# Earlier row loads, scatters in groups of four and later second-half gathers in a convolution-attention kernel

## The chip, the cores and the metric

The kernel runs on one core of a Trainium2 chip. A core has engines that run their own instruction streams: TensorE (PE; its weight loads are shown apart as PEld), VectorE (DVE), ScalarE (ACT) and GpSimd (POOL). SyncE (SP) issues most of the DMA transfers; ACT and POOL issue some. All of them wait for each other through semaphores. The metric is the device time of one launch in microseconds (us), the median of several runs.

## What is computed

The input `x` has 4 images of 32 channels, 128 x 128. Layer 0 is attention over channels: a space-to-depth step makes 128 x 4096 matrices `xs`, and

```
xs = space_to_depth(x)                       # per image: 128 channels, 4096 points
energy = einsum('bci,bcj->bij', q, q) / (d_i * d_j)      # 4096 x 4096, d: norms of the columns
out = gamma * einsum('bcj,bij->bci', q, softmax(energy)) + xs
```

Layer 1 works, image by image, on 4096 tokens of 128 numbers:

```
t = t + attention(layernorm(t))              # linear: Q (K^T V), summed over 8 heads
z = layernorm(t)
p = softmax(z @ router_w + router_b)         # 8 experts
top2, weights = top_k(p, 2), renormalised
t = t + sum_k weights[k] * (z @ expert_w[top2[k]] + expert_b)
```

All of it is in float32.

## The kernel before

**Images and steps.** The four images (0 to 3) run one after the other. `attend` walks the 4096 x 4096 score matrix of an image in tiles of 128 x 512, and only one triangle of it: row `i` of eight, columns `jc <= i`, four tiles each. One such tile is a **step**; an image has 144, counted here from 0 to 143. In a step PE makes the scores (L557, tile `pe`), ACT takes their exponent (L560, `pr`), PE multiplies an earlier `pr` with the values (L439, `po`), and the transposed share of an earlier tile is added with one more product (L374 or, for diagonal tiles, L395; `pg`). For that share DVE transposes 32 x 32 blocks (L368, L514, tile `F`) and the blocks are swapped by a trip through DRAM: SP issues one store (L482, L503) and six loads (L494). DVE adds the share to `o` (L384, L404).

**What is worked in between the steps.** The main loop keeps `clock`, which counts the work of the steps (12 for a full step; 4 to 10 for those of diagonal tiles), and `t`, the percentage of an image's 1568. It steps generators. Their instructions are put into the engines' queues in just this order, which is fixed for PE, DVE, ACT and SP; POOL's gathers, scatters and powers keep their program order as well.

- `prep(b, kc, st)` prepares a quarter `kc` of the rows of image `b`: it loads `xx` (four DMAs on SP, L278), transposes on PE into `ptq` (L312), copies to `qT` (L301, DVE), squares and sums (L323, L324), takes the power on POOL (`rn`, L163), scales (`qs`, L337) and transposes to `qn` (`ptn`, L345). It is listed in `timed` with a begin, an end and a count: in a step with `t` in reach it gets its next count if `done * (end - begin) < (t - begin) * count`. Each count resumes it twice, once before and once after the step's products. `idle(n)` yields 2n times, so n counts pass.
- `layer1(b, st)` of an image runs in the image after, in `steady`: one turn (two resumptions) per step, if `clock` has moved by 10 since its last turn. Image 3's is different: it has no sorting and finishes after the steps.

**Layer 1 in order.** `close_rows(kc)` divides the sums of a quarter of `o` (`den` L696, L701, PE `pbd` L723, L710, L732), takes the statistics (L735 and L631 to L637), a power on POOL (`rsa`, L163, and `nba`, L639), normalises on ACT (`xn`, L645) and adds to the Gram matrix (`pgram`, L677). The first quarter waits until the image before has set `sorted`. Then come `matrix`, `attention_rows` and `route`, and `sorted_experts(h)` for two halves of the tokens, which works in this order:

1. Scatter: 32 indirect DMAs of POOL write the half's token rows to `xs`, sorted by expert (L996), two to a turn. In half 1 two turns are left free after the 8th and after the 16th. Half 1 scatters when half 0 has "moved".
2. Products: after three free turns, pairs of tiles are loaded (L1022, SP), transposed (L1065), multiplied with the expert's weights (L1058, `pys`) and stored to `ys` (L1044, SP), in 25 turns. At their end half 1 sets `sorted`.
3. Gather: after one free turn, 32 indirect DMAs of POOL fetch the rows of `ys` into `yb` (L1123), two to a turn. Half 0 waits until half 1 has "moved", half 1 until half 0 has "gathered". Every fourth pair starts with a load of `acc` from DRAM on ACT's queue (L1099). DVE adds each gathered row four turns later (the combine, L1092), and every finished group of four is stored with four DMAs on SP (L1105).

Each scatter and gather also waits for the exponent of the step before it in the code (`wait_for(..., exps, ...)`), so that POOL doesn't run ahead. Counted in steps, half 0 scatters at 52 to 70, half 1 at 71 to 93; the products of half 0 go from 75 to 102, those of half 1 from 98 to 124; half 0 gathers at 104 to 121 and half 1 at 127 to 142. The `prep` calls of the next image load at steps 96 (`kc` 0) and 127 (`kc` 1) and transpose first at 101 and 130; `kc` 2 and 3 load at steps 4 and 47 of their own image.

The loop that paces it, as it stands (from L1339 on):

```
if b + 1 < B:
    nxt = states[b + 1]
    timed.append((prep(b + 1, 0, nxt), 65, 82, 13))
    timed.append((prep(b + 1, 1, nxt), 87, 99, 13))
...
        t = 100 * (clock[0] - start) / UNITS
...
        for n, (steps, begin, end, count) in enumerate(timed):
            if t >= begin and done[n] * (end - begin) < (t - begin) * count:
                moved.append(steps)
                done[n] += 1
```

Of the kernel before, what the change touches and what calls it, by code (L numbers as in the profile page):

```python
# [22 lines left out]
def kernel(  # L23
# [45 lines left out]
    B, C, H, W = x.shape  # L69
# [92 lines left out]
    def pow_neg_half(dst, src):  # L162
        pinned(nc.gpsimd.tensor_tensor(dst, src, neg_half.to_broadcast(list(src.shape)), ALU.pow))  # L163
# [13 lines left out]
    def idle(n):  # L177
        for _ in range(2 * n):
            yield

    def keep_running(n, pool=None, tag=None):

        bank = psum_t("spare") if pool is None else pool.tile([P, CH], F32, tag=tag, name="spare")
        for _ in range(n):
            nc.tensor.transpose(bank[:, :P], ident, ident)
# [4 lines left out]
    def hold(name, evict, alloc=psum_t):  # L190


        while len(held) >= banks[0]:
            held[0]()
        bank = alloc(name)

        def done():
            if done in held:
                held.remove(done)
                evict(bank)  # L200

        held.append(done)
        return bank, done
# [69 lines left out]
    def load_tokens(dst, b, k0, nk, queues=(nc.sync, nc.sync)):  # L273
        src = tokens(x, b)
        for r1 in range(2):
            for s in range(2):
                p0 = s * 64 + r1 * 32
                queues[r1].dma_start(dst[p0 : p0 + 32], src[s, r1, :, k0 : k0 + nk, :])  # L278


    def prep(b, kc, st):

        if b == 0:
            if kc == 0:
                st["all"] = big1.tile([P, 4, 8, HW2, 2], F32, tag="T", name="xx_0")
            xx = st["all"][:, kc]
        else:
            xx = xin.tile([P, 8, HW2, 2], F32, tag="xx", name=f"xx_{b}_{kc}")
        first = b == 0 and kc == 0
        load_tokens(  # L290
            xx.rearrange("p k w r -> p k (w r)"), b, 8 * kc, 8, (nc.sync, nc.scalar if first else nc.sync)
        )
        qT = qpool.tile([P, 2, NJ, P], F32, tag="qT", name=f"qT_{b}_{kc}")
        st.setdefault("qT", {})[2 * kc] = qT[:, 0]
        st["qT"][2 * kc + 1] = qT[:, 1]
        yield
        yield
        yield from idle(2 if b else 1)

        def load_half(g, pt):  # L300
            nc.vector.tensor_copy(  # L301
                qT[:, :, 2 * g : 2 * g + 2, :].rearrange("p s j (r c) -> p (j r) s c", c=64),
                pt.rearrange("p (m s c) -> p m s c", s=2, c=64),
            )

        for g in range(2):
            yield
            pt, done = hold(f"ptq_{b}_{kc}_{g}", partial(load_half, g))
            for jj in range(2):
                for r2 in range(2):  # L310
                    k = 4 * g + 2 * jj
                    nc.tensor.transpose(  # L312
                        pt[:, ts(2 * jj + r2, P)], xx[:, k : k + 2, :, r2].rearrange("p k w -> p (k w)"), ident
                    )
            yield
            done()
        yield
        yield
        ss = stat.tile([P, 2 * NJ], F32, tag="ss", name=f"ss_{b}_{kc}")
        rn = stat.tile([P, 2 * NJ, 1], F32, tag="rn", name=f"rn_{b}_{kc}")  # L320
        for s in range(2):
            sq = work.tile([P, NJ, P], F32, tag="qs", name=f"sq_{b}_{kc}_{s}", bufs=2)
            nc.vector.tensor_tensor(sq, qT[:, s], qT[:, s], ALU.mult)  # L323
            nc.vector.tensor_reduce(ss[:, ts(s, NJ)], sq, AX.X, ALU.add)  # L324
            if first:
                pow_neg_half(rn[:, ts(s, NJ), 0], ss[:, ts(s, NJ)])
            elif s == 1:
                pow_neg_half(rn[:, :, 0], ss)
            yield
            yield  # L330
        yield from idle(1)
        if first:
            keep_running(22, ps_g, "pg")
        scaled = []
        for s in range(2):
            qs = work.tile([P, NJ, P], F32, tag="qs", name=f"qs_{b}_{kc}_{s}", bufs=2)
            nc.vector.tensor_tensor(qs, qT[:, s], rn[:, ts(s, NJ)].to_broadcast([P, NJ, P]), ALU.mult)  # L337
            scaled.append(qs)
        for s, qs in enumerate(scaled):
            yield  # L340
            qn = npool.tile([P, CH], F32, tag="qn", name=f"qn_{b}_{2 * kc + s}")
            st.setdefault("qn", {})[2 * kc + s] = qn
            pt, done = hold(f"ptn_{b}_{kc}_{s}", lambda p, qn=qn: nc.scalar.activation(qn, p, AF.Copy))  # L343
            for j in range(NJ):
                nc.tensor.transpose(pt[:, ts(j, P)], qs[:, j, :], ident)  # L345
            yield
            done()
        yield
        yield
# [253 lines left out]
    def layer1(b, st):  # L603
# [9 lines left out]
        place = stat.tile([P, 2, KT], U32, tag="place", name=f"place_{b}", bufs=1)  # L613
        begin = stat.tile([P, 2, NT + 1], U32, tag="begin", name=f"begin_{b}", bufs=1)
        turns = [[], []]
        gate = first
        t2 = dram.tile([P, KT, D], F32, tag="t2", name=f"t2_{b}")
        keep = {}
# [302 lines left out]
        def sorted_experts(h):  # L921
# [66 lines left out]
            def offset(ap):  # L988
                return bass.IndirectOffsetOnAxis(ap=ap, axis=0)
# [4 lines left out]
            for n in range(2 * HR):  # L994
                k, i = r0 + n // 2, n % 2
                inst = nc.gpsimd.indirect_dma_start(xs[h], offset(place[:, i, k : k + 1]), xn[:, k, :], None)  # L996
                if not scatters:
                    pinned(inst)
                else:
                    tc.declare_no_dep(inst.ins, group=f"scatter_{b}_{h}", reason="no two tokens have the same place")  # L1000
                tc.add_to_no_dep_group(f"scatter_{b}_{h}", inst.ins)
                wait_for(inst.ins, xs_made[h] + xs_read[h], "what is replaced was made and read before")
                wait_for(inst.ins, exps, "not more of these at a time than steps have")
                scatters.append(inst.ins)
                if n % 2:
                    yield
                    yield
                if h == 1 and n in (7, 15):
                    yield from idle(2)
            turns[h].append("moved")  # L1010
            xs_made[h][:], xs_read[h][:] = scatters, []
# [68 lines left out]
                done()  # L1080
            if h == 1:
                st["sorted"] = True
            yield from idle(1)
            while "gathered" not in turns[0] if h == 1 else "moved" not in turns[1]:
                yield from idle(1)

# [244 lines left out]
    timed = [(first, 0, 1, 4)]  # L1331
    for b in range(B):

        if b == 0:
            for kc, begin, end in ((1, 0, 5), (2, 6, 20), (3, 25, 45)):
                timed.append((prep(0, kc, states[0]), begin, end, 12))
            timed.append((setup_weights(), 46, 58, 9))
            timed.append((setup_sorting(), 58, 98, 17))
        if b + 1 < B:  # L1339
            nxt = states[b + 1]  # L1340
            timed.append((prep(b + 1, 0, nxt), 65, 82, 13))
            timed.append((prep(b + 1, 1, nxt), 87, 99, 13))
        begin, end, count = (52, 94, 17) if b == 0 else (36, 47, 9)
        timed.append((input_rows(b, states[b]), begin, end, count))
        done = [0] * len(timed)
        start = clock[0]
        closing = None
        for half, _ in enumerate(chain(attend(b, states[b]), finish() if b == B - 1 else ())):
            if half % 2 == 0:
                t = 100 * (clock[0] - start) / UNITS  # L1350
                moved = []
                if closing is None and t > 84:
                    closing = layer1(b, states[b])
                    steady.append([closing.first_parts() if b == B - 1 else closing.all_parts(), clock[0]])
# [4 lines that stand above are left out]
                for stream in steady:  # L1359
                    if clock[0] >= stream[1]:  # L1360
                        stream[1] = clock[0] + PACE
                        moved.append(stream[0])
            for steps in moved:
                next(steps, None)
        for steps, *_ in timed:
            for _ in steps:
                pass
        timed = []
        if b + 1 < B:
            timed.append((prep(b + 1, 2, nxt), 2, 20, 13))  # L1370
            timed.append((prep(b + 1, 3, nxt), 30, 50, 13))
# [43 lines left out]
```

## Time and profile before

| what | us |
|---|---|
| median of 6 runs (1695.23 to 1698.42) | 1696.48 |
| the profiled execution's own time | 1699.35 |
| its span, first to last instruction | 1697.6 |
| PE busy in it | 1648.8 |
| DVE busy | 935.1 |
| ACT busy | 928.3 |
| POOL busy | 512.1 |
| first products of images 0, 1, 2, 3 | 13.8, 362.4, 767.6, 1171.2 |
| waits of PE for `xx` from DRAM (L312): 3, the longest | 11.5, 5.8 |
| waits of PE for `qs` of DVE (L345): 3, the longest | 7.8, 3.1 |
| waits of POOL's gathers (L1123) for a store of `ys` | 96.9 and 15.6 |

The mean granted clock of PE is 0.992 of full speed. 16 DMA engines moved 323.94 MB, a mean of 191 GB/s.

How to read it: the page gives the busy time of each engine, the span in 40 slices, the chain of work that ended last (each piece followed back to what released it) and the costliest groups of instructions. The timeline lists instructions in order of time: start, duration, engine, line, operation, output and input, and in brackets how long the engine stood idle before it and what ended that. The table by windows gives, for each stretch, its length, the busy time of PE, PEld, DVE, ACT and POOL with the number of instructions, the granted clock of PE (PEclk), the DMA share and GB/s. Times are us from the span's start. A product in float32 shows as two instructions.

### The profile page before, as it was taken

The numbers are of one execution on the slowest core, as the hardware profiler recorded it, in microseconds if no ns is written. First come the engines' busy times: TensorE is split into PE (matmuls) and PEld (weight loads), VectorE is DVE, ScalarE is ACT, GpSimd is POOL, SyncE is SP. The second block draws the span as 40 slices with busy tenths as digits, with TensorE's granted clock in tenths as the row PEclk, the third lists the DMA queues.
The fourth block names the chain that finished last, engine by engine and source line by source line (L and its number), as shares of the span: only waits on it lengthen the run. The fifth ranks groups of instructions, "written<-read, shape, count | busy, mean of one in ns | idle before, by whom it ended". The sixth has DMA issues, their size and how long they took to land.

```text
span 1697.6 us, 21941 instructions
## 1 busy us (share of the span) xinstructions
PE 1648.8 (97%) x5458; PEld 876.2 (52%) x5458; DVE 935.1 (55%) x2443; ACT 928.3 (55%) x2893; POOL 512.1 (30%) x553
## 2 busy tenths in 40 slices
PE   7999999999999999989999999999999999999898
PEld 4444444455554555545564455544555455554543
DVE  4434334467485335477468334557748633455686
ACT  3555445566565555546565555545557555554376
POOL 1000000011027425461014641544102742445167
PEclk9999999999999999999999999999999999999999
DMA  4554756754459778875457777886435876885001
GB/s 129 175 172 163 203 173 213 245 198 161 140 169 280 225 234 248 243 219 174 147 176 226 242 229 240 249 263 196 164 132 174 283 225 218 254 248 146 7 10 41
DMA packets 227341, 323.94 MB, mean 191 GB/s; under 512 B 31760, under 2 KB 155792, under 8 KB 213136
## 3 DMA queue, kind: packets, MB, share of 16 engines
q1 hardware_dynamic: 206704, 283.57, 52.8%
q0 software_dynamic: 12288, 25.19, 5.2%
q10 hardware_dynamic: 8224, 13.77, 2.8%
q8 instruction: 46, 0.75, 0.2%
q14 instruction: 79, 0.65, 0.1%
HBM read 152.28 MB, written 173.15 MB: 192 GB/s over the span
## 4 chain that ended last, share of the span: by engine, by line
PE 82%; DVE 7%; DMA 3%; ACT 3%; SPq 2%; issue 1%; POOL 1%; ACTq 0%; DVEq 0%; POOLq 0%
PE po L439 23%; PE pe L557 23%; PE pg L374 19%; PE pys L1058 3%; PE py L1207 2%; PE pg L395 2%; PE pys L1065 2%; PE pat L803 1%; PE pgram L677 1%; DMA F<-blocks 1%; ACT xn L645 1%; SPq L475 1%; PE ptq L312 1%; DVE F L368 1%; DVE df L710 1%
## 5 line engine op out<-in xcount | busy, mean ns | idle before, releaser
L560 ACT ACTIVATE pr<-pe 128x512 f32<-128x512 f32 (+1 forms) x576 | 322.6, 560 | 542.3 <-PE pe L557 501.3
L439 PE MATMUL po<-pr,qT 128*128 128x512 f32 (+3 forms) x1152 | 551.8, 561 | 3.9 <-ACT o L444 3.4
L557 PE MATMUL pe<-qn,qn 128*128 128x512 f32 x896 | 461.2, 596 | 2.0 <-ACT pr L560 1.7
L374 PE MATMUL pg<-F,qT 128*128 128x512 f32 x864 | 442.5, 594 | 1.9 <-DMA F<-blocks 1.2
L368 DVE STREAM_TRANSPOSE F<-pr 128x512 f32<-128x512 f32 x440 | 306.1, 702 | 150.4 <-ACT pr L560 137.3
L439 PEld LDWEIGHTS po<-pr,qT 128*128 128x128 f32 x1152 | 216.3, 191 | 250.9 <-issue 221.0
L379 ACT ACTIVATE junk<-F 128x512 bf16<-128x512 f32 x432 | 267.8, 620 | 2.1 <-DMA F<-blocks 1.3
L374 PEld LDWEIGHTS pg<-F,qT 128*128 128x128 f32 x864 | 164.4, 191 | 195.4 <-issue 178.5
L1123 POOL DMA_INDIRECT yb<-ys,place x192 | 186.0, 969 | 242.3 <-DMA ys<-xn 96.9
L996 POOL DMA_INDIRECT xs<-xn,place x192 | 186.1, 969 | 157.0 <-ACT pr L560 93.4
L557 PEld LDWEIGHTS pe<-qn,qn 128*128 128x128 f32 x896 | 154.3, 191 | 109.4 <-issue 101.6
L384 DVE TENSOR_TENSOR o<-o,pg 128x512 f32<-128x512 f32 x110 | 75.5, 686 | 205.7 <-PE pg L374 205.5
L163 POOL TENSOR_TENSOR rn<-ss,neg_half 128x8 f32<-128x8 f32 (+1 forms) x17 | 26.9, 1585 | 332.7 <-DVE ss L324 332.6
L560 ACT ACTIVATION_READ_ACCUMULATOR pr<-pe 128x1 f32 x576 | 111.9, 194 | 0.0
L1032 ACT ACTIVATE xn<-pys 128x256 f32<-128x256 f32 x120 | 45.3, 378 | 107.8 <-PE pys L1065 107.6
L163 POOL TENSOR_TENSOR rsf<-dm_f,neg_half 128x8 f32<-128x8 f32 (+1 forms) x15 | 26.2, 1748 | 233.7 <-DVE sv_f L637 233.7
L1058 PEld LDWEIGHTS pys<-ew_sb,xn 128*128 128x128 f32 x468 | 69.6, 191 | 46.5 <-issue 43.5
L557 PE MATMUL pe<-qn 128*128 128x512 f32 (+3 forms) x256 | 90.9, 438 | 0.7 <-ACT qn L343 0.7
L163 POOL TENSOR_TENSOR rsa<-dm_a,neg_half 128x8 f32<-128x8 f32 x16 | 26.4, 1649 | 192.0 <-DVE sv_a L637 191.6
L379 ACT ACTIVATION_READ_ACCUMULATOR junk<-F 128x1 f32 x432 | 82.6, 191 | 0.0
L1041 DVE COPY xn<-pys 128x256 f32<-128x256 f32 x60 | 25.4, 424 | 87.9 <-ACT xn L1032 86.4
L1041 DVE COPY result<-pys 128x256 f32<-128x256 f32 (+1 forms) x60 | 24.6, 410 | 88.2 <-ACT xn L1032 82.9
(216 smaller groups left out, 1670.8 us busy)
## 6 DMA issues: line engine op xcount, KB each, us to landing
blocks<-F SPq DMA_DIRECT2D x108, 1024.0 KB
F<-blocks SPq DMA_DIRECT2D x216, 192.0 KB
F<-blocks SPq DMA_DIRECT2D x216, 128.0 KB
xn<-xs SPq DMA_DIRECT2D x114, 128.0 KB
F<-blocks SPq DMA_DIRECT2D x216, 64.0 KB
below<-F SPq DMA_DIRECT2D x31, 384.0 KB
out_dram<-acc SPq DMA_DIRECT2D x128, 64.0 KB
xx<-in_x_dram SPq DMA_DIRECT2D x62, 128.0 KB
```

The lines of the kernel that those rows point to most:

```text
L163: pinned(nc.gpsimd.tensor_tensor(dst, src, neg_half.to_broadcast(list(src.shape)), ALU.pow))
L368: f()
L374: nc.tensor.matmul(pg.rearrange("p (a f) -> p a f", a=4), st["qT"][i][:, ib, :], G[:, :, ib], start=(ib == 0), stop=(ib == NJ - 1),)
L379: nc.scalar.activation(junk, G[:, :, ib], AF.Copy, accum_out=st["sums"][:, NJ * i + ib, jc : jc + 1])
L384: nc.vector.tensor_tensor(o, o, pg.rearrange("p (a j c) -> p a j c", a=4, c=S), ALU.add)
L439: nc.tensor.matmul(row["po"][:, lo:hi], qT[blk // NJ][:, blk % NJ, :], w, start=start, stop=(row["left"] == 0))
L557: nc.tensor.matmul(pe[:, c0:], qn[jc][:, ts(j, P)], qn[i][:, c0:], start=True, stop=True)
L560: nc.scalar.activation(pr[:, c0:], pe[:, c0:], AF.Exp, accum_out=sums[:, t, i : i + 1]).ins
L996: inst = nc.gpsimd.indirect_dma_start(xs[h], offset(place[:, i, k : k + 1]), xn[:, k, :], None)
L1041: nc.vector.tensor_copy(result[:, :n], p[:, 2 * P : 2 * P + n * D].rearrange("p (j c) -> p j c", c=D))
L1058: nc.tensor.matmul(p[:, 2 * P + j * D : 2 * P + j * D + D], bufs[4 + g % 2][:, j, :], weights[:, bass.ds(begins[2 * (g % 2) + j], D)], sta ...
L1123: inst = nc.gpsimd.indirect_dma_start(yb[k // 4][:, i, k % 4, :], None, ys, offset(place[:, i, k : k + 1]))
```

## The change

The whole diff:

```diff
@@ prep
         yield
         yield
-        yield from idle(2 if b else 1)
+        yield from idle((6 if kc < 2 else 2) if b else 1)
@@ layer1
         turns = [[], []]
+        paced = b < B - 2
         gate = first
@@ sorted_experts, scatter
                 if n % 2:
                     yield
                     yield
-                if h == 1 and n in (7, 15):
+                if paced and n % 4 == 3:
+                    yield from idle(1)
+                elif h == 1 and n in (7, 15):
                     yield from idle(2)
@@ sorted_experts, before the gather
             if h == 1:
                 st["sorted"] = True
-            yield from idle(1)
+            yield from idle(4 if paced and h == 1 else 1)
             while "gathered" not in turns[0] if h == 1 else "moved" not in turns[1]:
                 yield from idle(1)
@@ main loop
-            timed.append((prep(b + 1, 0, nxt), 65, 82, 13))
-            timed.append((prep(b + 1, 1, nxt), 87, 99, 13))
+            timed.append((prep(b + 1, 0, nxt), 60, 82, 17))
+            timed.append((prep(b + 1, 1, nxt), 83, 99, 17))
```

It does three things. The first two quarters of the next image's rows begin four counts earlier and have four more counts between their load and their first transposes. In layer 1 of images 0 and 1 (which run in images 1 and 2) the scatters of both halves go in fours, with one free turn after each four; this replaces half 1's two pauses of two turns. And in the same two images the second half's gathers have four free turns ahead of them instead of one. No instruction is added or removed on any engine; layer 1 of images 2 and 3 keeps its own pacing.

## Prediction

> **What bounds the kernel now.** I read the page first: PE is busy for 1648.8 of 1697.6 us, and 82% of the chain that ended last is PE. So a transfer or a DVE operation counts only where PE stands still for it, and I listed the gaps between PE's instructions. After the start and before the last image's tail only four exceed 1.2 us: 3.49 and 3.07 us in image 1, 2.19 and 3.07 us in image 2, each time at the same two steps. The chain of waits through image 1's two (start, us, what):
>
> ```profile
> 710.53 0.87 PE pe L557 x2
> 711.43 4.46 DMA acc<-t
> 716.34 0.43 SPq L278
> ...
> 719.11 5.08 DMA xx<-in_x_dram
> 724.32 0.72 PE ptq L312 x4
> ...
> 748.08 0.61 DVE qs L337
> 748.74 0.66 PE ptn L345 x4
> ```
>
> Steps are score tiles, 0 to 143 in each image; a step begins with its product L557, and what stands in which step is counted from the code's order and matched with the trace, instruction by instruction. The load of the next image's rows (L278) is issued in the code at step 127 (PE at 710.4), but SP issues it at 716.34, after a wait that the chain puts down to the landing of a gather's `acc<-t`; it lands at 724.2, and the transposes of step 130 wait. Later the transposes of step 137 wait for `qs`, because DVE is full: in 742 to 749 it is busy 6.86 of 7 us. PE's timeline shows what one gap costs:
>
> ```profile
> 719.80 1.02 PE L374 MATMUL pg<-F,qT 128*128 128x512 f32 x2
> 724.32 0.72 PE L312 MATMUL ptq<-ident,xx 128*128 128x128 f32 x4 [3.49 <-DMA xx<-in_x_dram]
> 724.87 1.15 PE L557 MATMUL pe<-qn,qn 128*128 128x512 f32 x2
> 725.81 1.91 PE L439 MATMUL po<-pr,qT 128*128 128x512 f32 x2
> 730.47 1.02 PE L439 MATMUL po<-pr,qT 128*128 128x512 f32 x2
> ```
>
> The pair at 725.81 takes 1.91 us against 1.02: the granted clock (PEclk, the third figure from the end) is 0.61 there.
>
> ```profile
> 718.00:725.00 7.00, 3.51 (x12) 1.66 (x11) 0.01 (x1) 1.30 (x4) 4.46 (x5) 1.00 1.05 294
> 725.00:729.40 4.40, 4.40 (x10) 1.75 (x9) 3.20 (x7) 1.30 (x4) 1.92 (x2) 0.61 0.99 268
> ```
>
> So a stall is priced by step lengths, from one L557 start to the next. A full step takes 2.58 us (729.61 to 732.19), four transposes 0.47 or 0.44 more. Steps 130 and 131 of image 1 take 11.52 (718.09 to 729.61) and should take 6.10: **5.42** lost. Steps 137 and 138 take 10.57 (742.93 to 753.50) and should take 5.60: **4.97**. Image 2's same steps lose 4.09 and 4.83. Image 0, with no gather, loses nothing there. Together **19.3 us** of 1697.6.
>
> **Part 1: the loads.** `prep` gets two turns per count. The transposes come at turn 8 now and at turn 16 after, that is at count 4 (t > 87 + 3x12/13 = 89.77) and at count 8 (t > 83 + 7x16/17 = 89.59): both are step 130 (t = 90.05). The load goes from the first step with t >= 87 (127) to the first with t >= 83 (121; t = 83.42): six steps ahead of where it was, PE at 694.7 instead of 710.4. Its four issues (0.43 to 1.19 us) pass SP's F<-blocks, ys and out_dram issues of those steps. SP's issues lag their step's start in PE by 5 to 12.7 us there, and issue to landing was 7.9 us (716.3 to 724.2), so the rows are there by 715.3 at the latest, and the transposes wanted them at 720.8. The load of the first quarter moves from step 96 to 89 and is not waited for now. Value: -5.42 and -4.09, nothing in images 0 and 3. What passed SP before it now comes up to 3.3 us later; the tightest swapped tile behind it (F_1_7_1) is issued 5.4 us before its product, and steps 125 to 129 get longer by 0.66 us each because the products move there (below): nothing.
>
> **Part 2: the scatters.** Layer 1 of the image before has one turn per step; steps of diagonal tiles, which move the clock by less than 10, give none. 32 scatters take 24 turns instead of 16 (half 0) and 20 (half 1). Half 0's products and gathers come 8 turns later, half 1's products 12. The instructions are the same; the POOL issues (0.96 us + 0.30) were not waited for. In place of gathers and products of steps 104 to 127 I get the same mix at 113 to 137; its precedent in the trace, beside the first quarter's transposes at 101 to 115, left no PE gap over 0.2 us. Value: 0.
>
> **Part 3: the second half's gathers** start 8 + 4 + 3 = 15 turns later: not at step 127 but at 142, and run to step 20 of the next image; combines run from step 5 to 26 instead of 131 to 5 of the next image. Also `close_rows(0)` of the next layer waits for `sorted`, 12 turns later: its first row (L696) goes from step 133 to 138. From steps 133 to 137 this takes six combines (0.34 each), the four L710 (2.78), L732 (1.22), eight L735 (1.6) and more: at least 7 us of a DVE that was 3.07 us late. Value: -4.97 and -4.83.
>
> **What they meet.** This cover is given back at the head of the next image, where `prep(.,2)` and `close_rows(2)` and `(3)` run. POOL keeps program order, and this order at step 19 is `rn`, a pair of gathers, `rsa`. Now, without gathers:
>
> ```profile
> 813.27 1.64 POOL L163 TENSOR_TENSOR rn<-ss,neg_half 128x8 f32<-128x8 f32 x1 [15.69 <-DVE ss L324]
> 815.02 1.64 POOL L163 TENSOR_TENSOR rsa<-dm_a,neg_half 128x8 f32<-128x8 f32 x1
> 816.97 1.65 ACT L645 ACTIVATE xn<-T,nba,rsa 128x128 f32<-128x128 f32 x4 [0.69 <-POOL nba L639]
> 818.86 1.05 PE L677 MATMUL pgram<-xn 128*128 128x128 f32 x8
> ```
>
> The four `xn` end at 817.46 to 818.62, and the four products that read one each start from 818.86 to 819.53: the last has 0.91 us of slack. The pair costs POOL 2 x (0.96 + 0.30) = 2.52, from these rows:
>
> ```profile
> 716.42 0.95 POOL L1123 DMA_INDIRECT yb<-ys,place  x1 [0.30 <-issue]
> 717.68 0.96 POOL L1123 DMA_INDIRECT yb<-ys,place  x1 [0.30 <-issue]
> ```
>
> It waits behind `rn`, and `rn` waits for DVE, which is nearly full there (the third busy figure):
>
> ```profile
> 795.00:805.00 10.00, 10.00 (x48) 6.72 (x47) 7.77 (x21) 7.99 (x27) 1.93 (x3) 1.00 0.49 147
> 805.00:815.00 10.00, 10.00 (x28) 4.71 (x27) 9.63 (x27) 3.99 (x13) 1.64 (x1) 1.00 0.52 180
> 815.00:825.00 10.00, 10.00 (x43) 6.26 (x42) 4.19 (x13) 7.58 (x26) 1.84 (x2) 1.00 0.64 219
> ```
>
> Six pairs of combines (0.70 each, 4.2) come between 789 and 811; idle time of DVE that takes them up is 2.06 before L404 at 801.6, little else: DVE is about 2.2 us late at `ss`. Stall at that `pgram` (step 21): 2.52 + 2.2 - 0.91 = **3.8**. Bounds: 1.6 if DVE isn't late, 0 if the pair is not in that place, 6.0 if the combines ahead of `rsa` and slower gathers (1.50 at 745.2) add 2.2. I take 3.8, since the order and the full DVE are both in the rows. The restart at the lower clock cost 1.93, 1.90, 1.90 and 1.76 in the four stalls (loss less gap): **1.9**. And `close_rows(0)` now reaches its `pgram` at step 1 of the next image, which lasts only 0.87 us; its DVE rows added up from step 140 on bring the last `xn` about 0.6 us too late: **0.6** (0 to 2). New cost at one boundary 6.3, at two 12.6.
>
> A rule that speaks against the restart term is in the Trainium skill, "TensorE: Matmul & The Clock Gate", Part 1: the clock is halved after an idle window of some 3.4 us. The trace differs: a gap of 2.19 us in image 2 was followed by a granted clock of 0.66 (1128 to 1133). By the page none of these gaps below 3.4 us would be followed by a restart; with my 3.8 us the sum is the same by both, and at the bound of 1.6 us it would be 3.8 us better.
>
> **Sum** for the profiled execution: 1699.35 us (span 1697.6) - 19.3 + 12.6 = 1692.7. It is 2.9 above the median of the runs, 1696.48, so the median goes to 1689.8, or **1690**.
>
> **Rivals.** (a) The two stalls go and nothing takes their place: POOL has issued the pair before `rn`, or DVE has room. For it: image 0 to 1 shows the same close_rows without any stall. Against: the pair's order and 0.91 us of slack. -19.3: 1677, up to 1683 with small stalls. (b) **Slower**: at the head of the next image the collision that is seen now at step 127 comes back. The third quarter's load (issued at 780.1, transposes at 793.6) gets no longer lead, and `acc<-t` of the moved gathers now stands before it in SP's waits. At 7.9 us to landing it may be 5.6 us later than now; SP is 4.9 us behind PE there, so it decides from 10.5 us behind, and 12.7 was reached at step 128. Price 5.42 per boundary on top of my forecast: -19.3 + 12.6 + 10.8 = +4.1, 1701. (c) The load is issued earlier in the code but not in time, because SP is behind: it would need over 18 us of lateness (694.7 to 712.9), and 12.7 is the most seen; the 9.5 stay, and the sum is +2.8: 1699.
>
> **Chances.** Forecast 0.50 (1683 to 1697; above 1693.1 it is within 0.2%, about what a measurement of this kernel can tell from no change), (a) 0.26, (b) 0.20, (c) 0.04. Faster by over 0.2%: 0.36 of the forecast's 0.50 + 0.26 = 0.62. Within: 0.13 + 0.04 = 0.17. Slower: 0.01 + 0.20 = 0.21. The range takes in (a) and most of (b): 1676 to 1702.
>
> **What would show it.** Right: no gap before L312 at step 130 nor before L345 at step 137 of images 1 and 2; L278 issued some 15 us earlier; gathers of half 1 until 50 us into the next image; a PE gap before `pgram` L677 near step 21 there, its `xn` waiting for `nba`, with a pair L1123 between the two L163. Wrong: that gap is missing (then 1677), or there is one before L312 near step 10 (then 1701).

## The result, and the profile after

| | median, us | runs |
|---|---|---|
| before | 1698.40 (1692.88 to 1703.31) | 71 |
| after | 1698.78 (1694.45 to 1703.83) | 31 |

The ratio is 1.0002, with a 95% interval of 0.9996 to 1.0009: no change that can be measured. The profiled executions stand the same way: 1699.12 us after (span 1697.3) and 1699.35 before (span 1697.6). Part of the miss is the base: the 1690 was reckoned from the median of six runs, 1696.48; over 71 runs it is 1698.40. The rest is the forecast gain of 6.7 us, which did not come.

In the changed kernel the line numbers of `layer1` behind the scatter's new branch are three higher (gather L1126, combine L1095, row load L1025, `acc` load L1102), those ahead of it one higher (scatter L997, `xn` L646, `pgram` L678).

**The four old gaps are gone.** PE's timeline of the changed kernel at steps 129 to 131 of image 1 (start, us, what; in brackets the idle time before it and what ended it):

```profile
717.64 0.61 PE L1061 MATMUL pys<-ew_sb,xn 128*128 x4
719.65 0.44 PE L1068 MATMUL pys<-ident,xn 128*128 128x128 f32 x2 [1.40 <-DMA xn<-xs]
...
722.50 0.63 PE L312 MATMUL ptq<-ident,xx 128*128 128x128 f32 x4
```

The transposes of `xx` (L312) start without a wait; before, there were 3.49 us ahead of them. But one step earlier stands a wait that was not there: 1.40 us for `xn<-xs`, a row load of the second half's products, which now run in these steps. The load of 128 KB took 6.79 us (the chain of waits has it from 712.82), in a window (714 to 721) with a DMA share of 1.02 and 348 GB/s; the clock stays at 1.00 behind this gap (721 to 725.4), where it was 0.61 behind the old one. At step 137 the transposes L345 follow the product before them without a gap, and in image 2 it is the same:

```profile
744.71 1.02 PE L374 MATMUL pg<-F,qT 128*128 128x512 f32 x2
745.57 0.60 PE L345 MATMUL ptn<-ident,qs 128*128 128x128 f32 x4
```

**The head of image 2 pays, as predicted.** POOL's timeline after, at steps 19 to 21:

```profile
810.84 1.71 POOL L163 TENSOR_TENSOR rn<-ss,neg_half 128x8 f32<-128x8 f32 x1 [5.30 <-DVE ss L324]
812.73 1.01 POOL L1126 DMA_INDIRECT yb<-ys,place  x1 [0.19 <-issue]
814.05 0.95 POOL L1126 DMA_INDIRECT yb<-ys,place  x1 [0.30 <-DVE F L368]
815.02 1.82 POOL L163 TENSOR_TENSOR rsa<-dm_a,neg_half 128x8 f32<-128x8 f32 x1
```

The pair of gathers stands between the two powers. PE then waits 2.75 us for the last `xn`, and the L439 pair behind it takes 1.32 us instead of 1.02:

```profile
817.78 2.08 PE L678 MATMUL pgram<-xn 128*128 128x128 f32 x8 [2.75 <-ACT xn L646]
...
820.50 1.32 PE L439 MATMUL po<-pr,qT 128*128 128x512 f32 x2
```

By the table of windows DVE is full from 795 to 815 (9.82 and 9.60 of 10 us, where it had been 7.77 and 9.63). In the window after that PE, the first busy figure, has 7.25 us, and its clock is 0.83:

```profile
815.00:825.00 10.00, 7.25 (x32) 5.75 (x32) 3.54 (x14) 6.29 (x22) 4.08 (x4) 0.83 0.89 271
```

**Image 0 pays too, which was not predicted.** SP's timeline, first before, then after:

```profile
232.76 0.42 SPq L482 DMA_DIRECT2D blocks<-F  x1
233.23 8.66 SPq L278 DMA_DIRECT2D T<-in_x_dram  x4
242.05 3.76 SPq L494 DMA_DIRECT2D F<-blocks  x6
```

```profile
232.92 8.19 SPq L278 DMA_DIRECT2D xx<-in_x_dram  x4
241.21 0.40 SPq L482 DMA_DIRECT2D blocks<-F  x1
...
247.29 3.23 SPq L494 DMA_DIRECT2D F<-blocks  x6
```

The four `xx` issues of the load for image 1 take 8.19 us of SP, because they wait there for a transfer `xs<-in_x_dram` of ACT's queue (the chain of waits has 3.02 us of it from 237.76). The kernel before has the same stop, but in the load of `T`, which stands behind the store `blocks<-F`. The store `blocks<-F` of step 101's tile is issued 8.5 us later than before, its loads 5.2 us later, and PE stands still:

```profile
253.74 1.31 PE L374 MATMUL pg<-F,qT 128*128 128x512 f32 x2 [1.89 <-DMA F<-blocks]
254.84 1.92 PE L557 MATMUL pe<-qn,qn 128*128 128x512 f32 x2
```

**The balance.** The same products in both profiled executions, after less before, give by stretch:

| stretch | predicted, us | measured, us |
|---|---|---|
| image 0 | 0 | +3.3 |
| image 1, steps 125 to 143 among them | -10.4 | -9.0 |
| head of image 2 | +6.3 | +6.9 |
| rest of image 2 | -8.9 | -8.1 |
| head of image 3 | +6.3 | +7.1 |
| rest of image 3 and the end | 0 | -0.4 |
| sum | -6.7 | -0.2 |

### The profile page after: what moved, and what is told of

Its sections match the earlier page's. It is cut to its first block, busy times and chain, and to the rows that moved or that the text cites. A ratio compares the mean times of both kernels' runs of the same rounds, so it can differ in the third digit from the quotient of the medians.

```text
span 1697.3 us, 21930 instructions
## 1 busy us (share of the span) xinstructions
PE 1648.3 (97%) x5458; PEld 876.2 (52%) x5458; DVE 934.3 (55%) x2443; ACT 927.9 (55%) x2893; POOL 511.9 (30%) x553
## 4 chain that ended last, share of the span: by engine, by line
PE 77%; DVE 7%; DMA 7%; ACT 3%; SPq 3%; issue 2%; POOL 1%; ACTq 0%; DVEq 0%; POOLq 0%
PE po L439 22%; PE pe L557 21%; PE pg L374 18%; PE pys L1061 3%; PE py L1210 2%; DMA blocks<-F 2%; PE pg L395 2%; DMA F<-blocks 2%; SPq L494 2%; PE pys L1068 1%; PE pgram L678 1%; DMA xn<-xs 1%; PE pat L804 1%; DVE F L368 1%; SPq L475 1%
## 5 line engine op out<-in xcount | busy, mean ns | idle before, releaser
L439 PE MATMUL po<-pr,qT 128*128 128x512 f32 (+3 forms) x1152 | 550.6, 560 | 3.3 <-ACT o L444 2.9
L557 PE MATMUL pe<-qn,qn 128*128 128x512 f32 x896 | 459.6, 595 | 1.9 <-ACT pr L560 1.6
L439 PEld LDWEIGHTS po<-pr,qT 128*128 128x128 f32 x1152 | 215.8, 191 | 249.8 <-issue 219.8
L997 POOL DMA_INDIRECT xs<-xn,place x192 | 185.0, 964 | 222.3 <-ACT pr L560 164.6
L1126 POOL DMA_INDIRECT yb<-ys,place x192 | 186.5, 971 | 202.0 <-ACT pr L560 62.9
L557 PEld LDWEIGHTS pe<-qn,qn 128*128 128x128 f32 x896 | 153.0, 191 | 103.6 <-issue 96.7
L1061 PEld LDWEIGHTS pys<-ew_sb,xn 128*128 128x128 f32 x468 | 69.9, 191 | 48.5 <-issue 46.4
L557 PE MATMUL pe<-qn 128*128 128x512 f32 (+3 forms) x256 | 91.1, 439 | 0.7 <-ACT qn L343 0.7
L1061 PE MATMUL pys<-ew_sb,xn 128*128 x468 | 71.6, 274 | 0.0
```

Of the source, the lines that this page charges most:

```text
L439: nc.tensor.matmul(row["po"][:, lo:hi], qT[blk // NJ][:, blk % NJ, :], w, start=start, stop=(row["left"] == 0))
L557: nc.tensor.matmul(pe[:, c0:], qn[jc][:, ts(j, P)], qn[i][:, c0:], start=True, stop=True)
L1061: nc.tensor.matmul(p[:, 2 * P + j * D : 2 * P + j * D + D], bufs[4 + g % 2][:, j, :], weights[:, bass.ds(begins[2 * (g % 2) + j], D)], sta ...
L1126: inst = nc.gpsimd.indirect_dma_start(yb[k // 4][:, i, k % 4, :], None, ys, offset(place[:, i, k : k + 1]))
```

## The experiments

**The theory** at the start: each part has its own effect, as the prediction priced it, plus the two costs just seen. **The rival**: the parts stand in for each other; a gap goes when the gathers move, whatever is done to the load. In an expectation, A and B are that run's own. The runs came in three groups of four, each with runs of the kernel before beside it (medians 1707.73, 1708.23 and 1697.73 us); the first two groups ran on one chip, the third on another, and a kernel is compared with others of its chip alone. The kernel before has a trace from the recorded runs only, so its gaps and times below are from there. In the table the microseconds are differences of medians; the ratio, with its interval, need not be the quotient of the medians (0.9929 stands for 12.1 us where the medians differ by 13.8).

| kernel | scatters | gathers | loads | against before, us | ratio (95%) |
|---|---|---|---|---|---|
| the changed kernel | new | new | new | +0.4 | 1.0002 (0.9996 to 1.0009) |
| the same, again | new | new | new | +0.4 | 1.0009 (0.9997 to 1.0020) |
| loads only | old | old | new | +2.7 | 1.0013 (0.9998 to 1.0027) |
| scatters only | new | old | old | -8.0 | 0.9957 (0.9941 to 0.9974) |
| gathers only | old | new | old | -9.5 | 0.9945 (0.9933 to 0.9958) |
| loads and scatters | new | old | new | -7.3 | 0.9962 (0.9948 to 0.9975) |
| scatters and gathers | new | new | old | -1.8 | 0.9991 (0.9978 to 1.0004) |
| loads of image 1 as before | new | new | new from image 2 | -1.2 | 0.9992 (0.9976 to 1.0008) |
| one free turn at step 19 | new | new | new | -7.0 | 0.9959 (0.9945 to 0.9973) |
| pause of 9 turns | new | new | new | -8.2 | 0.9950 (0.9932 to 0.9968) |
| the same, old loads | new | new | old | -13.8 | 0.9929 (0.9907 to 0.9951) |
| pause of 12, scatters alone | new | old | old | -11.1 | 0.9936 (0.9924 to 0.9948) |
| pause of 16, scatters alone | new | old | old | -10.9 | 0.9942 (0.9928 to 0.9956) |

"New" is as in the change, "old" as in the kernel before; a pause is in the second half's gathers.

**The loads alone.**

```diff
-        paced = b < B - 2
+        paced = False
```

> Only part 1 of the change (the two loads); scatters and gathers keep their old turns. Theory A (the stalls are additive and each belongs to its own part): the gaps at steps 130/131 of images 1 and 2 go (-5.4 and -4.1), those at steps 137/138 stay (4.97 and 4.83), the heads of images 2 and 3 have no new gap, and image 0 shows the gap for the block tile at step 101 (+3.8): in all -5.7 us against the kernel before, about 1692.7. Theory B (the earlier load helps only because the paced scatters also took the acc<-t transfers out of its way): a gap before L312 at step 130 stays, and the time is -1 to +4 us against before.

Measured: +2.7 us, 1.0013 (0.9998 to 1.0027). Each is right in one half: the gap before L312 goes, as A has it, but its time doesn't come back, and the result lies in B's range. SP's timeline around the load, first in the kernel before, then with the loads alone:

```profile
709.45 2.75 SPq L494 DMA_DIRECT2D F<-blocks  x6
715.96 0.34 SPq L482 DMA_DIRECT2D blocks<-F  x1
716.34 3.25 SPq L278 DMA_DIRECT2D xx<-in_x_dram  x4
```

```profile
703.52 2.40 SPq L278 DMA_DIRECT2D xx<-in_x_dram  x4
...
716.13 2.66 SPq L494 DMA_DIRECT2D F<-blocks  x6
```

The load is issued at 703.5 and is in good time. But SP's stop before 716 us stays: the chain puts it down to the landing of `acc<-t`, now ahead of F<-blocks instead of ahead of the load. So PE waits for the block tile, at almost the same place:

```profile
721.78 1.10 PE L374 MATMUL pg<-F,qT 128*128 128x512 f32 x2 [2.58 <-DMA F<-blocks]
```

In image 2 that gap is 3.31 us; step 137 of image 1 now waits 4.78 us for `qs` (3.07 before), that of image 2 2.33. The wait belonged to the queue and not to the load.

The instruction records of the trace also show why SP waits for a transfer that ACT issued. The 1577 transfers that SP and ACT issue signal their landing on eight semaphores, 100 to 107, which this program gives out in turn; an issue first waits (1443 of them do so in the trace of the kernel before) until the transfer that had its semaphore before it has landed. In the kernel before, `acc<-t` (issued at 711.43) has 107. The eighth transfer after it in the program, the store `blocks<-F` just ahead of the load, has 107 again: it goes out at 715.96, 0.07 us after `acc<-t` has landed, and the load behind it. With the loads alone the first of the F<-blocks transfers has the semaphore of `acc<-t`. The stop in image 0 is of the same kind: the fourth `xx` issue has the semaphore of `xs<-in_x_dram`. So which instruction is stopped depends on the order of all these transfers, and a change that moves some of them moves the stop.

**The scatters and the later gathers, loads as before.**

```diff
-        yield from idle((6 if kc < 2 else 2) if b else 1)
+        yield from idle(2 if b else 1)
...
-            timed.append((prep(b + 1, 0, nxt), 60, 82, 17))
-            timed.append((prep(b + 1, 1, nxt), 83, 99, 17))
+            timed.append((prep(b + 1, 0, nxt), 65, 82, 13))
+            timed.append((prep(b + 1, 1, nxt), 87, 99, 13))
```

> Only parts 2 and 3 (free turns of scatters and second-half gathers); the loads stay where they were. Theory A: the gaps at steps 137/138 go (-9.8), steps 130/131 still wait for xx (about 9.5 stay), image 0 loses nothing, the heads of images 2 and 3 pay 7.0 each as in the changed kernel: +4 us against before, up to +7 if the wait for the products' own loads at step 129 is also there. Theory B (the late load was an effect of the second half's gathers alone): no gap at step 130 either, and the time is about -5 us against before.

Measured: -1.8 us, 0.9991 (0.9978 to 1.0004). B is right about the gap: at step 130 only 0.48 us in image 1 is left, none in image 2, with the load at its old place. Why it goes is seen with the scatters alone, below: SP still stops for an `acc<-t` in the middle of the load. The time is above B's -5, because the heads cost more on this chip than B had counted with: 3.83 and 3.90 us of gap at step 21, and 0.95 and 0.92 before `pgram` at step 14 (the expectations below call it step 12), where the recorded trace of the changed kernel had none.

**The changed kernel again**, as the base on that chip:

> The changed kernel once more, as the base for the others on this chip. Both theories: within 2 us of the kernel before, with a gap at step 101 of image 0 (1.5 to 2 us), gaps for the products' loads at step 129 (0.8 to 1.9) and before pgram at step 21 of images 2 and 3 (2.75 to 3.9).

Measured: +0.4 us, 1.0009 (0.9997 to 1.0020), with gaps of 1.80 us at step 101 of image 0, 1.25 and 0.31 at step 129, 3.92 and 3.90 at step 21, as expected. The earlier loads make it 2.8 us slower than the kernel just above (1708.67 against 1705.90).

**The scatters alone.** Beside the loads of before:

```diff
-            yield from idle(4 if paced and h == 1 else 1)
+            yield from idle(1)
```

> Only part 2, the free turns of the scatters; the loads and the free turn ahead of the second half's gathers are as before. Everything of layer 1 behind the scatters comes 8 to 12 turns later all the same, sorted too. Theory A (this shift alone takes the gathers' acc<-t out of the way of the load at step 127 and the combines out of the way of close_rows): gap at step 130 at most 0.5 us, none at step 137, no pair between rn and rsa at step 19, a gap of 1.5 to 2.5 us before pgram at step 21: -4 to -8 us against before. Theory B (the parts do what the prediction put down to each: scatters nothing, loads steps 130/131, later gathers steps 137/138): gaps of over 2 us at 130 and 137 stay, and the time is that of before within 2 us or more.

Measured: -8.0 us, 0.9957 (0.9941 to 0.9974): this run's A in the time, and with it the rival. Gaps at step 130 are 0.72 and 0.35 us, none is at step 137. That part had been put at zero. But A's reason for step 130 is not what the trace shows: `acc<-t` is not out of the load's way. The four issues of the load, which take 3.25 us in the kernel before, take 6.70, because the second one waits for an `acc<-t` of the first half's gathers, which have moved there:

```profile
707.89 6.70 SPq L278 DMA_DIRECT2D xx<-in_x_dram  x4
```

```profile
714.57 1.02 PE L557 MATMUL pe<-qn,qn 128*128 128x512 f32 x2
715.43 1.02 PE L439 MATMUL po<-pr,qT 128*128 128x512 f32 x2
716.29 1.02 PE L374 MATMUL pg<-F,qT 128*128 128x512 f32 x2
718.03 0.72 PE L312 MATMUL ptq<-ident,xx 128*128 128x128 f32 x4 [0.72 <-issue]
```

What hides the wait is work of PE. The products (L1061, L1068) now stand in steps 127 to 129 and make each 0.66 us longer, so step 130 begins 9.72 us after step 127 (704.85 to 714.57) and not 7.73: PE comes to L312 1.99 us later. The rows come 0.78 us sooner after step 127, and 3.49 - 1.99 - 0.78 = 0.72 is left. In image 2 they come 0.15 later: 2.19 - 1.99 + 0.15 = 0.35.

At step 137 two things add up as well. From the start of step 132, `qs` is there after 16.92 us instead of 19.07: `close_rows(0)`, whose DVE work stood ahead of it, begins only at 18.26 and not at 4.63 (the combines are nearly as many as before, 12 against 13 in steps 128 to 137). And PE, which has the products there too, comes for it at 18.23 instead of 16.05. Either alone would leave some 0.9 us of the 3.07.

POOL at the head of image 2 has no pair between the powers, and `rsa` waits 0.68 us for DVE's `sv_a`:

```profile
810.68 1.71 POOL L163 TENSOR_TENSOR rn<-ss,neg_half 128x8 f32<-128x8 f32 x1 [7.98 <-DVE ss L324]
813.07 1.64 POOL L163 TENSOR_TENSOR rsa<-dm_a,neg_half 128x8 f32<-128x8 f32 x1 [0.68 <-DVE sv_a L638]
```

The gap at step 21 is 1.86 us instead of 3.9. So with the scatters paced, the three further turns cost some 6 us (-8.0 against -1.8): in the code they move the last gathers from step 17 to step 20.

**The later gathers alone**, loads and scatters as before:

```diff
-                if paced and n % 4 == 3:
-                    yield from idle(1)
-                elif h == 1 and n in (7, 15):
+                if h == 1 and n in (7, 15):
                     yield from idle(2)
```

> Only part 3, the three more free turns ahead of the second half's gathers of images 0 and 1; scatters and loads as in the kernel before. Theory A (the shift by the scatters is what takes the stalls away; three turns are too few): the second half's products and sorted are where they were, close_rows still starts at step 133, the gathers run from step 130 to 146; a gap of over 2 us stays at step 137, and that at step 130 is small or stays; between -3 and +2 us against before. Theory B (the prediction's own split: the later gathers are what clears step 137): no gap at 137, -8 to -10 us.

Measured: -9.5 us, 0.9945 (0.9933 to 0.9958). A is right in what it says of step 137 (gaps of 2.24 and 2.25 us stay) and wrong in the time; B the other way round. What goes is the gap at step 130, which the prediction had not put down to this part. SP's timeline with the later gathers alone:

```profile
711.21 0.37 SPq L482 DMA_DIRECT2D blocks<-F  x1
711.62 3.57 SPq L278 DMA_DIRECT2D xx<-in_x_dram  x4
```

It is the queue's order of before, without the stop: the second half's first `acc<-t` comes three turns later. The load is issued 4.7 us sooner, and no PE gap is left there. The stop itself stays here too: at 723.0, behind the load, SP waits 4.1 us for `acc<-t` among the F<-blocks of a later tile, and PE doesn't feel it. And the heads of images 2 and 3, where the other versions pay, are as long as before: the last gathers come 10 us into image 2, ahead of the place where DVE is full.

**Loads and scatters**, with the one old free turn ahead of the gathers:

```diff
-            yield from idle(4 if paced and h == 1 else 1)
+            yield from idle(1)
```

> Parts 1 and 2 without part 3: earlier loads and paced scatters, one free turn ahead of the second half's gathers as before. Theory A (the earlier loads only cost, once the scatters are paced): the gap at step 101 of image 0 is there (3.3 to 3.8 us with its restart), small gaps at step 129, nothing gained at step 130; 3 to 6 us slower than the paced scatters alone (-8.0), that is -2 to -5 us against before. Theory B (the loads and the scatters help independently): at least as fast as the paced scatters alone, -8 us or better.

Measured: -7.3 us, 0.9962 (0.9948 to 0.9975), between the two expectations, and on another chip than the scatters alone, so that the 0.7 us between them can't be told from nothing. Its profile shows what A names: 1.76 us of gap at step 101 of image 0, and 2.50 us for a product's row load at step 129 of image 2. For B, that the loads help on their own, it gives nothing: step 130 has at most 0.72 us of gap in the runs without them either.

**The loads of image 1 as before**, all else as in the change:

```diff
-        yield from idle((6 if kc < 2 else 2) if b else 1)
+        yield from idle((6 if kc < 2 and b > 1 else 2) if b else 1)
...
-            timed.append((prep(b + 1, 0, nxt), 60, 82, 17))
-            timed.append((prep(b + 1, 1, nxt), 83, 99, 17))
+            timed.append((prep(b + 1, 0, nxt), *((60, 82, 17) if b else (65, 82, 13))))
+            timed.append((prep(b + 1, 1, nxt), *((83, 99, 17) if b else (87, 99, 13))))
```

> The changed kernel, but the loads of image 1, which are worked in image 0, are where they were before. Theory A (the gap for the block tile at step 101 of image 0 comes from the earlier load that stands before its transfers on SP): no gap at 251.8 us, image 1 starts 3.3 to 3.8 us earlier, everything after is as in the changed kernel: -3.8 us against the changed kernel, about 1695. Theory B (that gap is chance of one execution): no difference of over 1 us in the medians.

Measured: 1706.51 us, 0.9992 (0.9976 to 1.0008) against before, 2.2 us less than the changed kernel on that chip (1708.67, in the next group). The gap at step 101 is gone, so it is no chance: all six profiled kernels with the earlier loads have it (1.55 to 2.13 us), and none of the others. Its price is smaller than the 3.3 to 3.8 expected. In the changed kernel's trace on that chip a gap of almost the same length, 1.80 us at 251.41, is not followed by slow products: the next L557 pair takes 1.02 us, and not the 1.92 that stand at 254.84 above, behind 1.89 us.

**One free turn where the pair stood**, else the changed kernel:

```diff
                 if n % 2:
                     yield
                     yield
                     due()
+                if paced and h == 1 and n == 27:
+                    yield
+                    yield
+                    due()
```

> The changed kernel, with one more free turn after the 28th gather of the second half, so that no pair of gathers stands between the two powers rn and rsa on POOL at step 19 of images 2 and 3. Theory A (POOL's order is what delays rsa): rsa starts some 1.8 us earlier after its dm, the gap of 2.75 us before pgram at step 21 shrinks to 1 us or less and is no longer followed by a lower clock: -3 to -3.7 us at each of two boundaries, -6 to -7.4 us against the changed kernel, about 1692. Theory B (DVE is late there by itself): rsa only waits for dm, the gap stays above 2 us and the time stays within 1.5 us of the changed kernel.

Measured: 0.9959 (0.9945 to 0.9973) against before; 1700.77 us against the 1708.67 of the changed kernel, 7.9 less: theory A, a little above its range in the time, though the gap stays above A's 1 us. `rsa` starts 0.68 us after `rn` ends instead of 2.49 us, so the pair cost 1.8 us of delay, and the gap at step 21 is 1.84 us instead of 3.9. `rsa` now waits for DVE's `sv_a`.

**A pause in the gathers.** Nine free turns instead, so that no gather is issued while `close_rows` and `prep` fill DVE:

```diff
                     due()
+                if paced and h == 1 and n == 15:
+                    for _ in range(9):
+                        yield
+                        yield
+                        due()
```

> The changed kernel, with nine more free turns after the 16th of the second half's gathers: none is issued from about step 8 to 21 of images 2 and 3, and the last 16 and their combines come at steps 22 to 34, where DVE is busy 17 to 37% of the time. Theory A (DVE is full at steps 10 to 21, 9.5 to 9.8 us of 10, and this is the stall): the gap before pgram at step 21 falls below 0.7 us, nothing takes its place: -10 to -14 us against the changed kernel. Theory B (what is moved is late wherever it goes): at steps 22 to 35 gaps before pgv or pat of 2 us or more appear, and the gain is under 5 us.

Measured: 0.9950 (0.9932 to 0.9968); 8.6 us less than the changed kernel, less than A's 10 and more than B's 5. The gap at step 21 is gone in both images and nothing of B's comes at steps 22 to 35 (0.32 us before L651 at 861.6 us). In this profile the losses of the loads stay (2.13 us of gap in image 0, 0.92 and 1.47 at step 129).

**The same with the loads as before** (the diff of the second experiment and the pause):

> As the run before it, but with the loads where they were in the kernel before. Theory A (with the scatters paced, the earlier loads bring nothing; they cost 3.8 us in image 0 and 1 to 3 at steps 129): 4 to 6 us less than with the earlier loads, -14 to -18 us against the kernel before. Theory B (the loads are worth their place): gaps before L312 at step 130 come back, and it is no faster than with the earlier loads.

Measured: 1694.48 us against 1708.23, 0.9929 (0.9907 to 0.9951), 5.6 us less than with the earlier loads: A. POOL and DVE at the head of image 2:

```profile
807.22 1.63 POOL L163 TENSOR_TENSOR rn<-ss,neg_half 128x8 f32<-128x8 f32 x1 [14.61 <-DVE ss L324]
808.96 1.63 POOL L163 TENSOR_TENSOR rsa<-dm_a,neg_half 128x8 f32<-128x8 f32 x1
...
813.30 1.04 POOL L1126 DMA_INDIRECT yb<-ys,place  x1 [2.43 <-ACT pr L560]
```

```profile
815.00:825.00 10.00, 9.68 (x39) 5.50 (x38) 5.69 (x12) 5.76 (x21) 5.19 (x6) 1.00 0.60 176
825.00:835.00 10.00, 10.00 (x40) 5.85 (x39) 2.63 (x6) 4.66 (x13) 2.62 (x3) 1.00 0.39 118
```

`rsa` follows `rn` at once, the gathers come behind both, and PE is busy for 9.68 us from 815 to 825, at the full clock, where the changed kernel had 7.25 in the recorded trace and 6.47 on this chip, with a clock of 0.83 in both. DVE has room from 825 us on.

**Scatters alone with a pause**, first 12 turns after the 16th gather (the diff), then 16 turns after the 8th (`n == 7`, `range(16)`):

```diff
+                if paced and h == 1 and n == 15:
+                    for _ in range(12):
+                        yield
+                        yield
+                        due()
```

> Part 2 alone, and twelve free turns after the 16th of the second half's gathers, so that the other 16 come from step 22 on as in the two runs with a pause. Theory A (three more turns ahead of the gathers bring nothing): as the paced version with the pause and all three free turns, -13 to -15 us against before, with a gap of about 1 us before pgram at step 12 left. Theory B (the three turns matter for close_rows at step 138): a gap of over 1 us at steps 137 to 140 comes back and the gain is 2 us or more smaller.

> As the run before it, but the pause begins after the 8th of these gathers (16 free turns), so that 24 come from step 22 to 34 and their combines to step 38. Theory A (what is left at step 12, some 0.9 to 1.2 us before pgram, is DVE's work on combines too): that gap goes, 1 to 2.5 us better than with the pause after 16, -15 to -17 us against before. Theory B (combines beyond step 33 meet the attention rows, where DVE is 60 to 75% busy): new gaps before pat, ptx or ptf at steps 33 to 45, no gain or a loss of up to 3 us.

Measured: 0.9936 (0.9924 to 0.9948) and 0.9942 (0.9928 to 0.9956), -11.1 and -10.9 us. Neither can be told from the run before (scatters, later gathers and a pause): the intervals of the ratios overlap, and so they do with the later gathers alone. They were expected at -13 to -15 and -15 to -17; on this chip no gap over 0.7 us stands at step 14 in either. Of theory B for the first, a gap at steps 137 to 140, there is no trace. The longer pause brings one new gap of 1.61 us before `ptx` (L651) in image 2, as theory B has it. All of the pause versions with the old loads beat both kernels.

## Why the prediction was wrong

**Right:** what bounded the kernel (the gaps at 130/131 and 137/138), their price by step lengths, that all four would go, and that the pair of gathers between `rn` and `rsa` would make a new one at step 21. The load at step 130 was in good time, with more to spare than forecast: L278 went out at 692.4, 24 us earlier, where some 15 were expected. Of rival (b) there is no trace, no gap before L312 near step 10. Of (c) neither.

**Wrong, with the place:**

1. **"Nothing in images 0 and 3."** Image 0 lost 3.3 us. "The load of the first quarter moves from step 96 to 89 and is not waited for now" looked at who needs the load, and not at who stands behind it on SP. The four issues were priced at some 3.3 us of SP; they take 8.19 there, since the stop for `xs<-in_x_dram` moves into them; the last load of the tile behind them was issued 6.4 us ahead of its product before and 3.6 us after, and it landed 3.27 us after its issue (the chain of waits).
2. **"What passed SP before it now comes up to 3.3 us later ... nothing."** Two terms behind "nothing" were not: the second half's row loads at step 129 lost 1.6 and 1.0 us. The products were rightly seen to move there (0.66 us per step), but not that each needs its own load in time: the first of these went out only at 712.82, behind a product of PE, and took 6.79 us. The DMA engines are full there (share 1.02), but that this made it late isn't shown; the kernel before has a share of 0.99 from 650 to 660 and no gap in PE. This and the head's size below make up the rest of the table's difference.
3. **The head, 6.3 predicted, 6.9 and 7.1 measured.** The kind was right, the size a tenth low; its pieces were not as put. The pair costs 1.8 us and not 2.52, for DVE's lateness runs beside it: the gap is 2.75 where 3.8 was forecast. The 0.6 for the `pgram` at step 1 did not come: it follows without a wait. Against that stand the `pgv` that waits 0.79 us for `gram` three steps on, slower steps at the low clock, and 0.9 us of `pgram` that moved over the boundary. On a second chip the gap is 3.9.

These add up to some 6.9 us: 3.3 + 2.2 (shortfall in images 1 and 2) + 1.4 (heads); with -0.4 at the end they turn -6.7 into -0.2.

**Wrong in the split, which the sum didn't show.** "Part 2: Value: 0" is the step that fails hardest in the experiments: alone it is worth 8.0 us. Part 1, credited with 9.5, shows no gain alone (+2.7, interval -0.3 to +4.6), and with the other two it costs 2.8. Part 3, credited with 9.8, brings 9.5 alone, but mostly by the gap at step 130 and not the one at 137; after part 2 it costs some 6. That all four gaps went as forecast is therefore in part luck: the gaps were the right ones, but they were credited to the wrong parts. The error behind all three is one: each gap was given to the edit that touches the instruction which waits, while three things decide it together: where SP's stop falls, what DVE has to do, and how much work PE has of its own until then.

- At 130 the later gathers move the stop behind the load, and the earlier loads move it on to the block tile. The scatters leave it in the load and put 1.99 us of products ahead of L312. The prediction had these products in its text ("steps 125 to 129 get longer by 0.66 us each") and put them at nothing.
- At 137 the three turns of the gathers leave 2.24 us; the scatters take `close_rows(0)` away from DVE (2.15 us) and bring products (2.18 us). The prediction named `close_rows(0)`, but counted it to part 3; its 12 turns come from the scatters.

So part 2 alone, or part 3 alone, brings as much as the whole change was forecast to bring. Part 3 on top of part 2 loses most of it again at the heads, and the earlier loads on top of both lose the rest.

**Not settled:** why the head's gap is 3.9 us on one chip, and 2.75 in the recorded runs, whose chip isn't on record, with the same order on POOL.

## What to carry to other kernels

When a transfer is late, ask what its queue waited for just before it: moving the transfer ahead of that wait only passes the wait to the next in the queue, and whoever it is moved past gets its duration as a delay. Look too at what the waiting engine has to do until then: work moved ahead of the wait hides as much of it as it lasts. Price each part of a change alone, against the others already made; parts that remove the same stall don't add up, while what they cost remains. Work that has to go somewhere (here 32 gathers and their combines) is best put where the engine's busy share in the windows is low (DVE at 2.6 of 10 us from 825 us on), even if it has to be stopped and taken up again.

## What was not expected of the hardware

How much a gap costs beyond its own length is not settled by its length. Over the profiled executions here, between the start and the last image's tail, gaps of 1.85, 1.89, 2.19, 2.25, 2.33, 2.50 and 2.75 (twice) us were followed by products at the low clock (up to 1.9 us for a pair instead of 1.02), gaps of 1.84, 1.85 (in another kernel), 1.86 (twice), 2.13, 2.24, 2.58, 2.65 and 2.88 us were not, nor was any from 1.21 to 1.80. With the later gathers alone, the same gap in images 1 and 2:

```profile
742.68 0.66 PE L345 MATMUL ptn<-ident,qs 128*128 128x128 f32 x4 [2.24 <-DVE qs L337]
743.18 1.02 PE L557 MATMUL pe<-qn,qn 128*128 128x512 f32 x2
...
1139.86 0.96 PE L345 MATMUL ptn<-ident,qs 128*128 128x128 f32 x4 [2.25 <-DVE qs L337]
1140.62 1.92 PE L557 MATMUL pe<-qn,qn 128*128 128x512 f32 x2
```

After 2.24 us the next pair takes 1.02, after 2.25 us 1.92. So the 1.9 us that the prediction added to each new stall is a chance and not a fixed price for the gaps below 3 us seen here; all eleven from 3.07 to 4.78 us were followed by slow products. In the Trainium skill, "TensorE: Matmul & The Clock Gate", Part 1, the clock is halved after an idle window of about 3.4 us, and the window is free-running. That it doesn't start with the gap agrees with gaps of one length costing different amounts; that a whole window must be idle doesn't agree with 1.85 to 2.75 us being enough.

The second thing is the spread between chips: the kernel before took 1707.7 and 1708.2 us on one and 1697.7 on another, a difference as large as what the better versions here gained. Only ratios against the kernel before on the same chip can be compared.
